# Inside an attention chunk: residue outermost, key block innermost

## The chip, the cores and the metric

The kernel runs on one core of a Trainium2 chip. The metric is device time of one launch in microseconds; 3923.4 us is the median of three runs of the kernel before (3923.32 to 3928.79).

The engines named here are PE (matrix products), DVE (vector), ACT (activations), POOL (GpSimd) and SP, which here only issues transfers. SBUF is the working memory, PSUM the memory that PE writes its sums to.

## The reference

The program is a chain of four layers on an input of 4 x 1024 tokens of 128 features, each an attention-like part and a feed-forward part with a residual and a layer norm. The change lies in the attention of layer 1, which attends not over tokens but over the 64 channels within each head of each token:

```python
H, C = (16, 64)
Q = (x @ Wq + bq).reshape(b, s, H, C) * inv_sqrt_c
K = (x @ Wk + bk).reshape(b, s, H, C)
V = (x @ Wv + bv).reshape(b, s, H, C)
scores = jnp.einsum('bshq,bshk->bshqk', Q, K)
mask = jnp.triu(jnp.ones((C, C), dtype=bool), 1)
scores = jnp.where(mask, -jnp.inf, scores)
w = jax.nn.softmax(scores, axis=-1)
attn = jnp.einsum('bshqk,bshk->bshq', w, V)
return attn.reshape(b, s, HID) @ Wo + bo
```

Each score is the product of two numbers, q of channel `q` and k of channel `k`, for `k <= q`. For 4096 tokens, 16 heads and 64 x 65 / 2 pairs there is one product, one subtraction of a row maximum, one exponential, one product with v, and two sums over k: the denominators and the numerators. No matrix product makes the scores; they are elementwise work.

## The kernel before, in words

**Tiling of the attention.** There are 32 tiles of 128 tokens, each cut into two units of 64 tokens, 64 units in all. A unit puts 32 tokens times 4 residues on the 128 partitions, and two such sets (`S = 2`) beside each other. A key channel is written `k = 4 n + r`: `n` is the key block (0 to 15), `r` the residue (0 to 3, `R = 4`). The partition group `i` of 32 holds the keys of residue `i`. So an operation over 128 partitions treats four keys of one block at once, one in each partition group.

**Tiles.** `qr` holds the queries of a unit, copied to all four partition groups, as (s, head, 64 channels) on the free axis; `mr` holds the row maxima in the same way. `kvr` is a PSUM bank with keys and values of eight key blocks (`half` 0 or 1), innermost axis the block. `ringe` is one long SBUF tile used as a ring: each chunk of scores takes a piece and gives it back when its numerator sum is done. `den` and `num` are PSUM banks with the sums, as 8 heads x 64 channels; two head halves and two sets fill four groups of 32 partitions.

**Chunks.** The generator `feed` (line 894) goes through 17 chunks a unit, in the order of line 898. An "n" chunk takes key block n against all later queries `q >= 4 (n + 1)`, where no mask is needed. A "d" chunk (two a unit, `i` = 0 and 1) takes, for eight key blocks at once, the queries that lie in the same block as the keys: 32 (s, head) rows x 8 blocks x 4 query residues = 1024 elements a partition. In a d chunk the mask matters: a key of residue `i` counts only for query residues `r >= i`. It is applied as a bias column of the exponential, `beyond[:, r]`, which holds a large negative number in the partition groups that must not count; so a d chunk needs four exponentials of 256 elements, one for each `r`.

**What happens to a chunk.** `feed` issues the first product, `ringe = qr * k`, on DVE (line 935; two of the n chunks of a unit on POOL, line 933). The generator `rest` (line 949) then issues: the subtraction `ringe - mr` on POOL (line 963); the exponential in place on ACT (line 973 for d chunks, line 975 for the others); the den sum on PE (line 981), by `add_up`, which multiplies with a 0/1 matrix that adds the four partition groups, in four calls, into `den[.., q0 : q0 + nq]`; the second product `ringe * v` in place on DVE (line 986); and the num sum on PE (line 998) by the same `add_up`. Sums of chunks keep their order through counters.

Before the change a d chunk lies in the ring as (row, block n, residue r), with r innermost, the order in which `qr`, `mr`, `den` and `num` hold their channels. The exponential of one `r` then takes every fourth element.

**Other places named.** `maxima` (line 808) writes `lo` (lines 814 to 817), a PSUM bank, through an output pattern in which neighbouring elements of the matmul land four floats apart; `queries` (line 799) writes a bank of the same size in contiguous order.

**What sets the order.** Every engine call goes through a recording wrapper (line 60), which is why the profile gives all of them the line L60; groups are told apart by tiles. The generators of all layers are merged by a planner (`Order`, line 138): it keeps a modelled clock for each engine, a modelled duration for each call (`length`, line 90), and issues next whatever can start first. The other layers run as three chains beside the attention. In `length`, an ACT call with an SBUF operand whose innermost step is more than one element is charged 1.05 ns more an element (lines 114 and 115); DVE's terms (103 to 108) and POOL's (121 to 124) do not ask for the step, only for a step of zero on POOL. The engines execute their queues in the order thus written out.

Of the kernel before, what the change touches and what calls it, by code (L numbers as in the profile page):

```python
# [14 lines left out]
AF = mybir.ActivationFunctionType  # L15
# [5 lines left out]
P = 128  # L21
# [8 lines left out]
H, C, R, S, NK = 16, 64, 4, 2, 16  # L30
SH = S * H
# [106 lines left out]
class Order:  # L138
# [28 lines left out]
    def part(self, ap):  # L167
        n = self.owner(ap)
        cols, piece = self.halved.get(n, (0, 0))
        return f"{n} part {ap.offset % cols // piece}" if cols else n  # L170
# [149 lines left out]
class Model:  # L320
# [573 lines left out]
    def feed(self):  # L894

        order = [("d", 1), *(("n", n) for n in range(8, NK - 1)), ("d", 0), *(("n", n) for n in range(8))]
        f = lambda tt: tt.rearrange("p s h c -> p (s h) c")
        count = 0  # L900
        for unit in self.units:
            seen = set()
            for kind, i in order:
                half = i if kind == "d" else i // 8
                if half not in seen:
                    seen.add(half)
                    yield "DVE", self.when(
                        lambda: unit.get("ready") and unit["half"][half],
                        lambda: max(self.order.until(unit["kvr"][half]), self.order.until(unit["qr"])),
                    )  # L910
                kk, vv = (unit["kvr"][half][:, x].rearrange("p s h n -> p (s h) n") for x in (0, 1))
                if kind == "d":
                    sh = [P, SH, 8, R]
                    part = lambda tt: f(tt)[:, :, 32 * i : 32 * i + 32].rearrange("p a (n r) -> p a n r", r=R)
                    kk, vv = (z[:, :, :, None].to_broadcast(sh) for z in (kk, vv))
                    q0, nq = 32 * i, 32
                    shape = lambda tt: tt.rearrange("p (a n r) -> p a n r", n=8, r=R)
                else:
                    q0 = R * (i + 1)
                    nq = C - q0  # L920
                    sh = [P, SH, nq]
                    part = lambda tt: f(tt)[:, :, q0:]
                    kk, vv = (z[:, :, i % 8, None].to_broadcast(sh) for z in (kk, vv))
                    shape = lambda tt, nq=nq: tt.rearrange("p (a q) -> p a q", q=nq)
                shared = (kind, i) in SHARED
                yield "POOL" if shared else "DVE", self.when(
                    lambda: self.ering.can(SH * nq), lambda: self.ering.back(SH * nq)
                ), True
                et = self.ering.take(SH * nq)
                e = shape(et)  # L930
                qk = part(unit["qr"]), kk
                if shared:
                    self.g.tensor_tensor(e, qk[0], unit["ks"][i][:, :, None].to_broadcast(sh), ALU.mult)
                else:
                    self.v.tensor_tensor(e, *qk, ALU.mult)
                self.asked(unit)
                what = dict(first=(kind, i) == order[0], last=(kind, i) == order[-1], q0=q0, nq=nq, half=half)
                rest = self.rest(unit, count, kind, et, shape, part(unit["mr"]), vv, **what)
                self.order.spawn(rest, "rest", self.order.latest)
                count += 1  # L940

# [7 lines left out]
    def rest(self, unit, count, kind, et, shape, m, vv, first, last, q0, nq, half):  # L949
        e = shape(et)  # L950
        rows = et.rearrange("p (s h q) -> p s h q", s=S, q=nq)

        def add_up(name):
            for hb in range(2):
                for s in range(S):
                    at = 32 * (S * hb + s)
                    self.pe.matmul(
                        unit[name][at : at + 32, :, q0 : q0 + nq], lhsT=self.k["rep"][:, 0:32],
                        rhs=rows[:, s, 8 * hb : 8 * hb + 8, :], start=first, stop=last,
                    )  # L960

        yield "POOL"
        self.g.tensor_tensor(e, e, m, ALU.subtract)
        unit["subs"] -= 1
        if unit["subs"] == 0:
            self.drop(unit["mr"])
            if unit is self.units[-1]:
                self.retire("mr", "hc", "big")
        yield "ACT"
        if kind == "d":  # L970

            for r in range(R):
                self.s.activation(e[:, :, :, r], e[:, :, :, r], AF.Exp, bias=self.k["beyond"][:, r : r + 1])
        else:
            self.s.activation(et, et, AF.Exp)

        turn = lambda: self.summed == count
        yield "PE", self.free("den", also=turn) if first else self.when(turn)
        if first:
            unit["den"] = self.new("den", 8, C)  # L980
        add_up("den")
        self.summed += 1
        if last:
            self.order.spawn(self.invert(unit), "close", self.order.latest)
        yield "DVE", self.when(lambda: self.valued == count)
        self.v.tensor_tensor(e, e, vv, ALU.mult)
        self.valued += 1
        unit["uses"][half] -= 1
        if unit["uses"][half] == 0:
            self.drop(unit["kvr"][half])  # L990
            if unit is self.units[-1] and len(self.slots["kvr"]) == 2:
                self.retire("kvr", "bg")
                self.most = 3
        turn = lambda: self.done == count
        yield "PE", self.free("num", also=turn) if first else self.when(turn)
        if first:
            unit["num"] = self.new("num", 8, C)
        add_up("num")
        self.done += 1
        self.ering.give(self.order.latest)  # L1000
        self.order.place = self.done / (17.0 * 2 * TPG)
        if self.order.place == NG:
            self.divide(self.ering.ap, "b", "b", "c")
        if last:
            self.order.spawn(self.close(unit), "close", self.order.latest)
# [1080 lines left out]
```

## Time and profile before

| what | value |
|---|---|
| median of three runs | 3923.4 us |
| the profiled execution | 3929.3 us, its span 3927.5 us |
| mean granted TensorE clock | 0.912 |
| DVE busy over the span | 3167.7 us (81%) |
| PE busy | 3096.5 us (79%) |
| POOL busy | 2922.0 us (74%) |
| ACT busy | 2628.2 us (67%) |
| DMA, mean rate | 85 GB/s |

The span is the time from the first to the last instruction of one profiled execution; the median comes from runs of their own. A group row of the profile names line, engine, operation, the tile written, the tiles read and the shape, then busy time and the mean duration of one, then how long the engine was idle just before and what ended that idle time. A row of a tile's own view gives shortest, median and longest duration in ns. A row of waits gives who waited for whom, total us, how often, and the longest.

A d chunk in the trace, from 2013.98 us: DVE's product of 1024 elements, from 2015.28 POOL's subtraction, from 2017.70 ACT's four exponentials in 2.83 us, from 2019.05 eight matmul records of the den sum in 0.64 us, from 2019.83 DVE's second product in 1.22 us, and from 2021.97 the num sum in 0.62 us.

### The profile page before, as it was taken

The page shows a single profiled execution, that of the slowest core. Times are in us where ns is not written, and L with a number is a line of the kernel's source. Part 1 is how long each engine was busy: PE and PEld are TensorE (multiplying, and loading weights), DVE is VectorE, ACT ScalarE, POOL GpSimd, SP SyncE. Part 2 cuts the span into 40 slices and gives each one's busy share as a digit, 9 for nine tenths or more (in the row PEclk, how much of TensorE's full clock was granted, in tenths as well). Part 3 has the DMA queues.
Part 4 walks back from the last instruction along what each step waited for, and adds up shares of the span by engine and source line. Part 5 has one row for each costly group of instructions (what it writes and reads, how often), then busy time and mean ns, then how long its engine had stood idle before and what let it go on. Part 6 is the DMA issues. An engine that isn't in the chain of part 4 may idle for free.

```text
span 3927.5 us, 130511 instructions
## 1 busy us (share of the span) xinstructions
PE 3096.5 (79%) x56496; PEld 1636.6 (42%) x56496; DVE 3167.7 (81%) x3988; ACT 2628.2 (67%) x5206; POOL 2922.0 (74%) x1320
## 2 busy tenths in 40 slices
PE   5577676777788887978888987978878888879872
PEld 2233232433344553544444553544444444436552
DVE  2888898899898889899888889889998988983321
ACT  4567565667667875777667875677766786666531
POOL 0779996999788887799788987788978987870000
PEclk8789788988899998999999999999999999989986
DMA  2322122212213333243423334243433334523564
GB/s 68 80 72 50 44 57 61 63 44 52 50 50 100 84 95 82 75 119 80 103 70 94 97 87 99 61 109 87 108 88 75 94 94 102 140 74 81 162 151 99
DMA packets 374136, 334.05 MB, mean 85 GB/s; under 512 B 196332, under 2 KB 304172, under 8 KB 373560
## 3 DMA queue, kind: packets, MB, share of 16 engines
q1 hardware_dynamic: 364216, 292.15, 30.0%
q0 software_dynamic: 9344, 33.56, 2.9%
q8 instruction: 442, 7.24, 0.8%
q14 instruction: 134, 1.10, 0.1%
HBM read 149.16 MB, written 42.21 MB: 49 GB/s over the span
## 4 chain that ended last, share of the span: by engine, by line
PE 27%; DVE 25%; ACT 17%; POOL 16%; issue 10%; DMA 4%; SPq 1%; DVEq 0%; POOLq 0%; ACTq 0%
DVE ringe L60 17%; POOL ringe L60 15%; PE bg L60 14%; ACT ringe L60 8%; PE den L60 6%; PE num L60 5%; DVE bg L60 4%; PE kvr L60 2%; ACT ha L60 2%; ACT b L60 1%; ACT x L60 1%; DVE a L60 1%; SPq L60 1%; ACT L60 1%; DVE b L60 1%
## 5 line engine op out<-in xcount | busy, mean ns | idle before, releaser
L60 POOL TENSOR_TENSOR ringe<-ringe,mr 128x1024 f32<-128x1024 f32 (+14 forms) x1088 | 2558.0, 2389 | 466.1 <-DVE ringe L60 346.4
L60 DVE TENSOR_TENSOR ringe<-ringe,kvr 128x1024 f32<-128x1024 f32 (+14 forms) x1102 | 1291.3, 1202 | 201.6 <-PE den L60 183.4
L60 ACT ACTIVATE ringe<-ringe 128x768 f32<-128x768 f32 (+14 forms) x964 | 1001.2, 1056 | 593.7 <-POOL ringe L60 590.6
L60 DVE TENSOR_TENSOR ringe<-qr,kvr 128x1024 f32<-128x1024 f32 (+12 forms) x960 | 1102.3, 1184 | 60.1 <-PE num L60 31.2
L60 PE MATMUL den<-ringe,cst 128*32 128x256 f32 (+7 forms) x8744 | 700.8, 419 | 263.6 <-ACT ringe L60 215.5
L60 PE MATMUL num<-ringe,cst 128*32 128x256 f32 (+7 forms) x8728 | 702.7, 411 | 213.8 <-DVE ringe L60 204.2
L60 PEld LDWEIGHTS den<-ringe,cst 128*32 128x32 f32 x8744 | 238.8, 115 | 573.0 <-ACT ringe L60 353.5
L60 PEld LDWEIGHTS num<-ringe,cst 128*32 128x32 f32 x8728 | 233.6, 114 | 539.3 <-DVE ringe L60 399.7
L60 ACT ACTIVATE ringe<-ringe,cst 128x256 f32<-128x256 f32 x512 | 357.2, 782 | 64.2 <-POOL ringe L60 63.9
L60 POOL TENSOR_TENSOR ringe<-qr,ks 128x896 f32<-128x896 f32 (+1 forms) x128 | 288.3, 2252 | 48.0 <-DMA mr<-t 23.4
L60 PE MATMUL bg<-xT,a 128*32 128x512 f32 (+1 forms) x1952 | 253.3, 616 | 31.3 <-DMA a<-w 9.2
L60 DVE TENSOR_TENSOR_SCAN bg<-ends,bg 128x512 f32<-128x512 bf16 x128 | 154.9, 1217 | 44.9 <-PE bg L60 43.4
L60 PE MATMUL kvr<-wkv,xT 128*32 128x256 f32 x2048 | 149.6, 413 | 31.9 <-DVE ringe L60 30.6
L60 PE MATMUL bg<-a,ha 128*32 128x128 f32 x4736 | 160.2, 276 | 14.6 <-ACT ha L60 14.4
L60 PEld LDWEIGHTS bg<-a,ha 128*32 128x32 f32 x4736 | 127.8, 111 | 35.8 <-ACT ha L60 18.1
L60 ACT COPY b<-bg 128x512 f32<-128x512 f32 (+2 forms) x217 | 96.6, 452 | 57.3 <-PE bg L60 53.1
L60 PE MATMUL bg<-xT,b 128*32 128x128 f32 (+1 forms) x3536 | 128.4, 285 | 8.2 <-ACT aT L60 4.8
L60 ACT ACTIVATE ha<-bg,cst 128x512 f32<-128x512 f32 (+1 forms) x151 | 97.6, 678 | 52.8 <-PE bg L60 52.6
L60 ACT ACTIVATE b<-cst,little 128x128 f32<-128x128 f32 x384 | 122.2, 397 | 0.0
L60 PEld LDWEIGHTS bg<-xT,b 128*32 128x32 f32 x3536 | 102.3, 114 | 35.3 <-issue 14.8
L60 PEld LDWEIGHTS bg<-xT,a 128*32 128x32 f32 x1952 | 61.5, 116 | 131.1 <-issue 61.2
L60 PE MATMUL bg<-b,cst 128*32 128x512 f32 (+1 forms) x800 | 107.4, 608 | 1.6 <-ACT b L60 0.9
(660 smaller groups left out, 4450.5 us busy)
## 6 DMA issues: line engine op xcount, KB each, us to landing
qr<-q SPq DMA_DIRECT2D x512, 128.0 KB
mr<-t SPq DMA_DIRECT2D x512, 128.0 KB
c<-in_f_Wdn SPq DMA_DIRECT2D x53, 256.0 KB
tu<-gt SPq DMA_DIRECT2D x25, 512.0 KB
c<-tu SPq DMA_DIRECT2D x200, 64.0 KB
td<-gt SPq DMA_DIRECT2D x24, 512.0 KB
c<-td SPq DMA_DIRECT2D x96, 128.0 KB
a<-in_f_W SPq DMA_DIRECT2D x37, 256.0 KB
```

Of the source, the lines that this page charges most:

```text
L60: return f(*args, **kw)
```

## The change

In a d chunk the element order in the ring becomes (row, residue r, block n), with n innermost. The exponential of one `r` then takes runs of eight neighbouring elements. `qr`, `mr`, `den` and `num` keep their order; so the d chunk's product reads `qr`, and its subtraction reads `mr`, with a step of four floats (16 bytes) between neighbours, and the two sums write `den` and `num` with that step. `kvr` is read with the block innermost and a repeat over r, where before the repeat was innermost. The n chunks are as they were. The planner's `length` is untouched.

```diff
                 if kind == "d":
-                    sh = [P, SH, 8, R]
-                    part = lambda tt: f(tt)[:, :, 32 * i : 32 * i + 32].rearrange("p a (n r) -> p a n r", r=R)
-                    kk, vv = (z[:, :, :, None].to_broadcast(sh) for z in (kk, vv))
+                    sh = [P, SH, R, 8]
+                    part = lambda tt: f(tt)[:, :, 32 * i : 32 * i + 32].rearrange("p a (n r) -> p a r n", r=R)
+                    kk, vv = (z[:, :, None, :].to_broadcast(sh) for z in (kk, vv))
                     q0, nq = 32 * i, 32
-                    shape = lambda tt: tt.rearrange("p (a n r) -> p a n r", n=8, r=R)
+                    shape = lambda tt: tt.rearrange("p (a r n) -> p a r n", n=8, r=R)
...
         rows = et.rearrange("p (s h q) -> p s h q", s=S, q=nq)
+        turned = (lambda t: t.rearrange("p h (n r) -> p h r n", r=R)) if kind == "d" else (lambda t: t)
...
                     self.pe.matmul(
-                        unit[name][at : at + 32, :, q0 : q0 + nq], lhsT=self.k["rep"][:, 0:32],
+                        turned(unit[name][at : at + 32, :, q0 : q0 + nq]), lhsT=self.k["rep"][:, 0:32],
                         rhs=rows[:, s, 8 * hb : 8 * hb + 8, :], start=first, stop=last,
                     )
...
             for r in range(R):
-                self.s.activation(e[:, :, :, r], e[:, :, :, r], AF.Exp, bias=self.k["beyond"][:, r : r + 1])
+                self.s.activation(e[:, :, r], e[:, :, r], AF.Exp, bias=self.k["beyond"][:, r : r + 1])
```

## The prediction

> **What bounds the kernel now.** I began with busy time by engine over the stretch in which the attention runs (its ring tile is written from 102 to about 3520 us), because the last 400 us hold other layers and would blur the shares.
>
> ```profile
> core 0: us, PE busy (x) PEld busy (x) DVE busy (x) ACT busy (x) POOL busy (x), PEclk, DMA share, GB/s
> 100.00:3520.00 3420.00, 2746.08 (x48483) 1397.75 (x48479) 3031.38 (x3587) 2400.09 (x4524) 2891.68 (x1279) 0.92 0.32 81
> ```
>
> In these 3420 us DVE is busy 88.6%, POOL 84.6%, PE 80.3%, ACT 70.2%. DVE is nearest to being the bound, POOL close behind, ACT has the most room. Next the waits and the last chain:
>
> ```profile
> ACT ringe L60 <- POOL ringe L60: 654.5, 446, 16.8
> POOL ringe L60 <- DVE ringe L60: 346.4, 94, 34.9
> DVE ringe L60 <- PE den L60: 195.1, 144, 5.4
> ```
> ```profile
> PE 27%; DVE 25%; ACT 17%; POOL 16%; issue 10%; DMA 4%; SPq 1%; DVEq 0%; POOLq 0%; ACTq 0%
> ```
>
> ACT waits for POOL, POOL waits for DVE, and DVE waits little, mostly for the den sum that must have read a chunk before DVE overwrites it. So DVE sets the pace, and a microsecond added to it counts nearly in full, while one saved on ACT counts only where DVE stands behind it. The chain passes through all engines, so no edit counts exactly at its own size.
>
> **The change, part by part.** There are 64 units with two d chunks each: 128 d chunks of 128x1024. No instruction is added or removed in kind: per chunk still one product on DVE, one subtraction on POOL, four exps on ACT, a den sum on PE, the second product on DVE, a num sum on PE. What changes is the step in bytes of their operands. Before, only the exps have a step of 16 bytes (every fourth float, read and written). After, the exps read and write runs of 8 floats; the first product reads qr every 16 bytes, the subtraction reads mr every 16 bytes, and the sums write den and num every 16 bytes. The rows:
>
> ```profile
> L60 ACT ACTIVATE ringe<-ringe,cst 128x256 f32<-128x256 f32 x512 | 357.2, 782 | 64.2 <-POOL ringe L60 63.9
> L60 ACT ACTIVATE ringe<-ringe 128x256 f32<-128x256 f32 x68 | 28.4, 418 | 10.4 <-POOL ringe L60 9.3
> L60 ACT ACTIVATE ha<-bg,cst 128x512 f32<-128x512 f32 x144 | 94.3, 688 | 52.3 <-PE bg L60 52.2
> L60 ACT ACTIVATE b<-bg 128x512 f32<-128x512 f32 x98 | 57.8, 592 | 27.3 <-PE bg L60 24.7 <-issue 1.8 <-ACT xp L60 0.7
> L60 DVE TENSOR_TENSOR ringe<-qr,kvr 128x1024 f32<-128x1024 f32 x192 | 231.1, 1211 | 37.8 <-ACT ks L60 28.5 <-PE num L60 9.1
> L60 DVE TENSOR_TENSOR ringe<-ringe,kvr 128x1024 f32<-128x1024 f32 x192 | 232.2, 1212 | 30.6 <-PE den L60 26.9 <-ACT ha L60 2.6 <-ACT last L60 0.2
> L60 POOL TENSOR_TENSOR ringe<-ringe,mr 128x1024 f32<-128x1024 f32 x192 | 456.4, 2391 | 73.1 <-DVE ringe L60 40.9 <-PE bg L60 13.0 <-PE num L60 10.9
> L60 POOL TENSOR_TENSOR ringe<-ringe,mr 128x1536 f32<-128x1536 f32 x64 | 222.8, 3482 | 2.7
> L60 POOL TENSOR_TENSOR ringe<-qr,ks 128x1536 f32<-128x1536 f32 x64 | 177.8, 2778 | 22.7 <-PE num L60 21.6 <-ACT x L60 1.0
> ```
>
> *ACT.* The strided exp takes 782 ns for 256 elements; a contiguous ringe activation of that size 418 ns without a bias column. A bias column costs 688 - 592 = 96 ns (the two PSUM rows). A contiguous exp with bias is then 514 ns, so the stride costs 268 ns, 1.05 ns for an element. 512 x 0.268 = 137 us leave ACT. Bounds: 0, if runs of 8 do no better, to 512 x (782 - 418) = 186 us. I take 137: nearly all of it is cover that ACT had. Its worth is bounded by the wait before the second product, 26.9 us behind den in the row above (64 other chunks share it).
>
> *DVE, first product.* No row of before has a DVE operand in SBUF with such a step. From below: 0, if DVE at 1211 / 1024 = 1.18 ns an element hides the fetch. From above: the only strided row there is, ACT's 1.05 ns an element, makes 1024 x 1.05 = 1.07 us a chunk and 128 x 1.07 = 137 us. ACT's excess may come from its strided write rather than its read, which the row cannot separate; but DVE's pace is as near to one element a step as ACT's (1811 ns for 1920 elements), so I see nothing that would hide a slower fetch, and take 137 us. The other operand in PSUM costs nothing either way: the broadcast moves from the innermost place to the one before it, and a DVE product that reads PSUM element by element (rd<-num,rd, 685 ns for 512) is as fast as one with an innermost broadcast (ringe<-ringe,kvr, 677 for 512). The second product is contiguous in ringe before and after: 0.
>
> *POOL, subtraction.* Again no row. Bounds 0 to ACT's 1.05 ns an element, 137 us. That POOL pays for operands one by one is seen in its rows: with one operand broadcast, 1536 elements take 2778 ns instead of 3482, 0.46 ns an element less. A slower fetch then shows, and I take 137 us. POOL goes to (2892 + 137) = 3029 us of busy time.
>
> [...]
>
> *PE.* The strided output has a row. The maxima's matmul writes its bank with the same 16-byte step (line 815), the queries' matmul writes 512 contiguous:
>
> ```profile
> L60 PE MATMUL bg<-wkv,xT x512: 591/592/1062, 87.5 to 3348.4; 128*32 128x512 f32 x171
> L60 PE MATMUL bg<-wq,xT x512: 591/592/1061, 78.7 to 3322.6; 128*32 128x512 f32 x171
> ```
>
> Shortest and median are equal: 0 on PE. It is cheap only while that holds; the rival below has the price.
>
> [...]
>
> *Order.* The planner drops its stride term (line 115) for the exps, 0.27 us each, and has no such term for DVE or POOL (lines 103 to 108, 121 to 124). So all five queues are reordered, SP's transfers among them, on durations that are about 1 us too short twice per d chunk; what stands behind a late product in DVE's queue (other chunks' products, scans, residual sums) is late with it, and POOL waits for it. I charge nothing for that and leave it in the width.
>
> **Sum.** DVE +137, less up to 27 that ACT's shorter exps take from its wait: +110. POOL's 137 goes beside it, since at 3029 of some 3530 us it stays at 86%, under DVE's 3168 (90%). On the profiled span: 3927.5 + 110 = 4037.5. That execution took 3929.3 and the median of three is 3923.4, so on the median 4033 us. From half the DVE price to the full one with 57 us of mistimed order behind it: 3975 to 4090 for this case alone.
>
> **Rivals.**
> - *Neither DVE nor POOL pays* (the end on the other side). ACT's excess is then its strided write, and after the change every write to SBUF is in runs. For it: DVE's writes are contiguous as before. Against it: ACT's row has both, and POOL pays visibly for operands. ACT loses 137 of 2628 us; of its 17% of the chain (668 us) that share is 35 us, and the wait behind den gives 27. I take -20: 3903, and 3888 at most. It decides as soon as a strided 128x1024 product stays under about 1.3 us.
> - *POOL alone pays.* POOL reaches 3029, DVE's present 3031, so both stand at 88.6%. POOL's wait for DVE (346 us) takes up about half: +69, less the 20 from ACT: about 3972.
> - *The sums on PE pay too*: the change does move a stride where accumulating cost may differ from the maxima's single write. One sum of a d chunk takes 0.62 us in the timeline; twice that on 256 sums is +159 us on PE, 2905 of busy time. Half of it on the path on top of the forecast: about 4113. Against it are the two equal rows.
>
> **How the numbers follow.** The forecast (DVE pays, POOL with it or not) 0.64; POOL alone 0.13; PE too 0.05; neither 0.18. A measurement of this kernel tells about 0.2% (7.8 us) from no change. Of the neither case 0.13 is faster by more, 0.04 within, 0.01 slower because of the new order; all else is slower: 0.83. The range is 3910 to 4090: below lie most of the neither case (0.11), above the PE case and the forecast's upper tail (0.09).
>
> **What would show it.** Exp on ringe<-ringe,cst near 514 ns; of the qr,kvr 128x1024 group a third (its 192 mix 128 d and 64 n chunks) still at 1.21 us and the rest near 2.28, mean near 1.9; the ringe,mr 128x1024 group's mean near 3.1; den and num 128x256 unchanged near 0.41; DVE's share of the attention's stretch near 90% and that stretch near 3530 us. The forecast is wrong if the DVE product stays at 1.21, or if DVE's added time appears and the stretch does not grow.

## The result and the profile after

The changed kernel takes 3934.61 us (median of 10 runs, 3931.51 to 3938.57) against 3927.84 us for the kernel before (10 runs): ratio 1.0021, 95% interval [1.0011, 1.003]. It is slower by 6.8 us, where 110 were forecast. The profiled execution took 3933.5 us with a span of 3931.8.

First the groups whose operands changed their step, in the view of groups by shape of the changed kernel:

```profile
L60 ACT ACTIVATE ringe<-ringe,cst 128x256 f32<-128x256 f32 x512 | 218.0, 499 | 109.4 <-POOL ringe L60 109.2
L60 DVE TENSOR_TENSOR ringe<-qr,kvr 128x1024 f32<-128x1024 f32 x192 | 338.6, 1767 | 31.7 <-ACT ks L60 17.5 <-PE num L60 11.9 <-DMA mr<-t 2.2
L60 DVE TENSOR_TENSOR ringe<-ringe,kvr 128x1024 f32<-128x1024 f32 x192 | 233.1, 1216 | 17.9 <-PE den L60 14.2 <-ACT ringe L60 2.1 <-ACT bg L60 0.8
L60 POOL TENSOR_TENSOR ringe<-ringe,mr 128x1024 f32<-128x1024 f32 x192 | 526.9, 2755 | 124.4 <-DVE ringe L60 110.9 <-PE den L60 4.4 <-DMA qr<-q 3.1
L60 PE MATMUL den<-ringe,cst 128*32 128x256 f32 x1536 | 131.5, 416 | 76.5 <-ACT ringe L60 53.0 <-ACT rd L60 5.8 <-POOL ringe L60 4.9
```

An exponential fell from 782 to 499 ns: 512 x 0.283 = 145 us less on ACT. The qr,kvr group mixes 128 d chunks with 64 n chunks; with the n chunks at their old 1211 ns, a d product takes (192 x 1767 - 64 x 1211) / 128 = 2045 ns, 0.83 us more, 107 us on DVE. A subtraction takes (192 x 2755 - 64 x 2391) / 128 = 2937 ns, 0.55 us more, 70 us on POOL. The second product reads its `kvr` operand with the repeat moved in the same way, and it kept its duration (1216 ns, before 1212); so the 0.83 us belong to the step in `qr`. The sums kept theirs within 5 ns. So every part moved in the direction forecast, yet the total hardly did. Busy time in the same 3420 us of the attention, by engine as in the prediction's first table:

```profile
core 0: us, PE busy (x) PEld busy (x) DVE busy (x) ACT busy (x) POOL busy (x), PEclk, DMA share, GB/s
100.00:3520.00 3420.00, 2734.38 (x48365) 1389.94 (x48357) 3116.36 (x3561) 2266.02 (x4502) 2949.66 (x1275) 0.92 0.32 81
```

DVE is busy 3116 us there (91.1%, before 88.6%), POOL 2950, ACT 2266. In the same stretch DVE is busy 85 us longer, in time in which it was idle before. How far the attention itself grew is seen from when the last first product of a unit starts, in the tile's own view of before and then of the changed kernel:

```profile
L60 DVE TENSOR_TENSOR ringe<-qr,kvr x960: 269/1210/2153, 102.0 to 3513.7; 128x1024 f32<-128x1024 f32 x64, 128x256 f32<-128x256 f32 x64, 128x1664 f32<-128x1664 f32 x64
L60 DVE TENSOR_TENSOR ringe<-qr,kvr x960: 261/1347/2203, 102.3 to 3532.1; 128x1024 f32<-128x1024 f32 x64, 128x256 f32<-128x256 f32 x64, 128x1664 f32<-128x1664 f32 x64
```

It starts 18 us later, where some 110 were forecast, and the rest of the program behind it takes 400 us against 414. The waits say where some of DVE's time went:

```profile
ACT ringe L60 <- POOL ringe L60: 746.9, 520, 9.3
POOL ringe L60 <- DVE ringe L60: 307.9, 94, 12.4
DVE ringe L60 <- PE den L60: 141.4, 134, 4.0
```

DVE waits 141 us for den sums, before 195; POOL waits 308 us for DVE, before 346; ACT waits 747 us for POOL, before 655. The chain of the changed kernel is traced over only 56% of its span, so its shares can't be set beside those of before:

```profile
PE 19%; DVE 13%; ACT 8%; POOL 7%; issue 5%; DMA 3%; SPq 1%; DVEq 0%; POOLq 0%; ACTq 0%
```

### The profile page after: what moved, and what is told of

Its sections match the earlier page's. It is cut to its first block, busy times and chain, and to the rows that moved or that the text cites. A ratio compares the mean times of both kernels' runs of the same rounds, so it can differ in the third digit from the quotient of the medians.

```text
span 3931.8 us, 130457 instructions
## 1 busy us (share of the span) xinstructions
PE 3087.4 (79%) x56496; PEld 1630.5 (41%) x56496; DVE 3269.1 (83%) x3988; ACT 2502.5 (64%) x5206; POOL 2991.7 (76%) x1320
## 4 chain that ended last, share of the span: by engine, by line
PE 19%; DVE 13%; ACT 8%; POOL 7%; issue 5%; DMA 3%; SPq 1%; DVEq 0%; POOLq 0%; ACTq 0%
PE bg L60 11%; DVE ringe L60 9%; POOL ringe L60 7%; PE den L60 4%; PE num L60 3%; ACT ringe L60 3%; DVE bg L60 2%; PE kvr L60 2%; ACT b L60 1%; SPq L60 1%; ACT ha L60 1%; ACT L60 1%; ACT x L60 0%; DMA mr<-td 0%; DVE b L60 0%
## 5 line engine op out<-in xcount | busy, mean ns | idle before, releaser
L60 POOL TENSOR_TENSOR ringe<-ringe,mr 128x1024 f32<-128x1024 f32 (+14 forms) x1088 | 2627.2, 2451 | 399.6 <-DVE ringe L60 307.9
L60 DVE TENSOR_TENSOR ringe<-qr,kvr 128x1024 f32<-128x1024 f32 (+12 forms) x960 | 1211.7, 1298 | 58.7 <-PE num L60 38.9
L60 PEld LDWEIGHTS num<-ringe,cst 128*32 128x32 f32 x8728 | 225.6, 113 | 570.5 <-DVE ringe L60 450.3
L60 ACT ACTIVATE ringe<-ringe,cst 128x256 f32<-128x256 f32 x512 | 218.0, 499 | 109.4 <-POOL ringe L60 109.2
L60 PE MATMUL bg<-b,cst 128*32 128x512 f32 x832 | 110.6, 604 | 5.0 <-ACT b L60 4.9
```

The lines of the kernel that those rows point to most:

```text
L60: return f(*args, **kw)
```

## The experiments

The change does two things at once: it moves the step between engines, and it lets the planner write a new order. All experiments rest on keeping these apart. A flag around the four exponentials tells the planner what to charge for them, whatever their real step is; nothing else in it looks at what the change touches. With 1 it charges the old term and gives every queue the old order, instruction by instruction; with 2 it charges none and gives the order of the changed kernel. The traces bear this out: in every run said to be in one of the two orders the queues of DVE, ACT, POOL and SP hold the same instructions in the same order, and PE's agree in over 99.5% of their places. The runs with one part alone mix up elements and are no usable kernels; they serve to price the part.

```diff
-        if any(not in_psum(a) and a.free_size() > 64 and a.ap[-1][0] > 1 for a in aps[:2]):
+        if BEYOND[0] == 1 or BEYOND[0] == 0 and any(not in_psum(a) and a.free_size() > 64 and a.ap[-1][0] > 1 for a in aps[:2]):
             long += 1.05e-3 * n
...
+            BEYOND[0] = 1
             for r in range(R):
...
+            BEYOND[0] = 0
```

Before was run again beside each group of runs: 3928.7 us for the first four, 3925.5 for the next, 3927.9, 3924.8 and 3924.5 for the others. Ratios are against it.

### Layout and order apart

> The changed layout with every queue in the order of the kernel before (the planner still charges the four exponentials of a d chunk with their old stride term). Theory 'order': the new layout alone costs what the prediction said and the new order gave it back: +60 to +110 us over before. Theory 'trade': the layout's loss on DVE and POOL is paid back by ACT's gain whatever the order: within 15 us of before. Theory 'slack': DVE's added time fits into its own idle time: also within 15 us, told apart from 'trade' by the two runs with one part alone.

3969.2 us, ratio 1.0102 [1.0088, 1.0117]: +40 us. The last first product starts at 3557.5 us, 44 later than before. The layout alone costs far more than the change did, less than theory "order" said and more than "trade" and "slack" allowed.

> The layout of before with every queue in the order of the changed kernel (the planner no longer charges the stride term for the four exponentials, which still pay it on the chip). Theory 'order': the new order is the better one, so 50 to 100 us below before. Theories 'trade' and 'slack': the order is worth little, within 15 us of before (a few us slower, since ACT's time is now underrated by 1.1 us a chunk).

3923.4 us, ratio 0.9991 [0.9981, 1.0001]: with the old layout the new order can't be told from the old one. With the new layout it is worth 3969.2 - 3934.6 = 35 us.

### One part at a time, in the old order

ACT alone:

```diff
-                self.s.activation(e[:, :, :, r], e[:, :, :, r], AF.Exp, bias=self.k["beyond"][:, r : r + 1])
+                run = et.rearrange("p (a r n) -> p a r n", n=8, r=R)[:, :, r]
+                self.s.activation(run, run, AF.Exp, bias=self.k["beyond"][:, r : r + 1])
```

> In the order of before, only the four exponentials take runs of eight; products, subtractions and sums stay as before, so biases meet elements of other residues and the output is not the reference's. ACT should lose 0.28 us x 512 = 145 us of busy time, DVE and POOL nothing. Theory 'trade': 30 to 70 us faster than before. Theory 'slack': ACT's time was cover, 0 to 10 us faster.

3896.7 us, ratio 0.9918 [0.9905, 0.9931]: 32 us faster. ACT's time was not only cover. But the wait from which the prediction took its worth, the second product's behind den, fell only from 26.9 to 22.3 us:

```profile
L60 DVE TENSOR_TENSOR ringe<-ringe,kvr 128x1024 f32<-128x1024 f32 x192 | 233.5, 1218 | 28.5 <-PE den L60 22.3 <-ACT ringe L60 3.0 <-ACT ha L60 2.1
```

POOL's wait for DVE fell more, from 346 to 318 us.

DVE alone, on the first product of d chunks (written in more lines here than in the kernel):

```diff
+                if kind == "d":
+                    q, k = unit["qr"].rearrange("p s h c -> p (s h) c")[:, :, q0 : q0 + 32], unit["kvr"][half][:, 0].rearrange("p s h n -> p (s h) n")
+                    qk = q.rearrange("p a (n r) -> p a r n", r=R), k[:, :, None, :].to_broadcast([P, SH, R, 8])
+                    e = et.rearrange("p (a r n) -> p a r n", n=8, r=R)
```

> In the order of before, only the first product of a d chunk reads qr with the 16-byte step (and kvr with the repeat outside); subtraction, exponentials and sums take the elements as before, so they are mixed up and the output is not the reference's. DVE should gain 0.83 us x 128 = 107 us of busy time. Theory 'trade': 40 to 107 us slower than before. Theory 'slack': DVE hides it, 0 to 15 us slower.

3964.6 us, ratio 1.0092 [1.0079, 1.0105]: +36 us. The group of this run shows the full price on the engine:

```profile
L60 DVE TENSOR_TENSOR ringe<-qr,kvr 128x1024 f32<-128x1024 f32 x192 | 338.4, 1770 | 35.9 <-ACT ks L60 26.4 <-PE num L60 9.4
```

107 us more on the engine that is busiest, and 36 us more in the end. Both theories had this outside or at the edge of what they said: the part is neither hidden nor counted in full.

POOL alone, on the subtraction:

```diff
-        self.g.tensor_tensor(e, e, m, ALU.subtract)
+        if kind == "d":
+            m = m.rearrange("p a n r -> p a r n")
+            ee = et.rearrange("p (a r n) -> p a r n", n=8, r=R)
+            self.g.tensor_tensor(ee, ee, m, ALU.subtract)
+        else:
+            self.g.tensor_tensor(e, e, m, ALU.subtract)
```

> In the order of before, only the subtraction of a d chunk reads mr with the 16-byte step; the other steps take the elements as before, so they are mixed up and the output is not the reference's. POOL should gain 0.55 us x 128 = 70 us of busy time. If the parts add up to the new layout in the old order (+40 of which DVE +36 and ACT -32), POOL alone is 25 to 45 us slower than before. If POOL hides behind DVE, as the prediction had it, 0 to 10 us slower and the parts don't add up.

3958.7 us, ratio 1.0088 [1.0071, 1.0105]: +33 us for 70 us of busy time.

```profile
L60 POOL TENSOR_TENSOR ringe<-ringe,mr 128x1024 f32<-128x1024 f32 x192 | 526.8, 2757 | 75.9 <-DVE ringe L60 50.2 <-PE bg L60 11.4 <-ACT a1nm L60 11.2
```

POOL does not hide behind DVE.

PE alone, den and num of d chunks through `turned`:

> In the order of before, only the den and num sums of the d chunks are written with the 16-byte step in PSUM (the sums go to channels of other residues, so the output is not the reference's). Theory 'free', by the equal rows of the maxima's and queries' matmuls: den and num 128x256 unchanged near 0.41 us, time within 5 us of before. [...]

3930.0 us, ratio 1.0009 [0.9999, 1.0019]: +4 us, and by the interval between 0 and 7. The groups of the d and n chunks together:

```profile
L60 PE MATMUL den<-ringe,cst 128*32 128x256 f32 x1536 | 132.6, 416 | 72.1 <-ACT ringe L60 34.8 <-ACT last L60 13.1 <-ACT ks L60 11.7
L60 PE MATMUL num<-ringe,cst 128*32 128x256 f32 x1536 | 127.6, 404 | 36.7 <-DVE ringe L60 31.4 <-DVE rd L60 4.4
```

Before they were 411 and 402 ns. But in the run with DVE alone, whose sums are written without a step, they were 416 and 406:

```profile
L60 PE MATMUL den<-ringe,cst 128*32 128x256 f32 x1536 | 132.1, 416 | 64.0 <-ACT ringe L60 33.9 <-ACT last L60 14.4 <-ACT ks L60 6.1
L60 PE MATMUL num<-ringe,cst 128*32 128x256 f32 x1536 | 128.2, 406 | 45.3 <-DVE ringe L60 40.4 <-DVE rd L60 4.3
```

So the step in PSUM costs nothing that can be seen here.

The four parts add up: 36 + 33 - 32 + 4 = 41 us, and the layout as a whole cost 40. So they do in the attention: its last first product moves by 40, 32, -32 and 5 us, 45 in all, against 44.

### Where on DVE the step is paid

The changed kernel, with this in place of the first product's operands (again in more lines than in the kernel):

```diff
+                if kind == "d":
+                    q, k = unit["qr"].rearrange("p s h c -> p (s h) c")[:, :, q0 : q0 + 32], unit["kvr"][half][:, 0].rearrange("p s h n -> p (s h) n")
+                    qk = q.rearrange("p a (n r) -> p a n r", r=R), k[:, :, :, None].to_broadcast([P, SH, 8, R])
+                    e = et.rearrange("p (a r n) -> p a n r", n=8, r=R)
```

> The changed kernel in its own order, but the first product of a d chunk goes through its elements as before: it reads qr contiguously with the repeat of kvr innermost, and writes ringe with a step of 8 floats (32 bytes). Nothing is left out. Theory 'read pays': the product is back at 1.21 us and the kernel 25 to 45 us below the changed kernel, at 3890 to 3910. Theory 'write pays too': the product stays near 2.0 us or above and the time within 10 us of the changed kernel's 3935.

3931.1 us, ratio 1.0016 [1.0005, 1.0026]: no gain over the changed kernel that can be told.

```profile
L60 DVE TENSOR_TENSOR ringe<-qr,kvr 128x1024 f32<-128x1024 f32 x192 | 333.7, 1742 | 28.2 <-ACT ks L60 17.6 <-PE num L60 7.6 <-DMA qr<-q 2.7
```

A d product takes (192 x 1742 - 64 x 1211) / 128 = 2008 ns. A write with a step of 32 bytes costs DVE 0.80 us, as much as a read with 16 (0.83).

### What an order is worth

The planner told of DVE's and POOL's real price:

```diff
-        return long, 0.14
+        return long + (0.81e-3 * n if any(not in_psum(a) and a.free_size() > 64 and a.ap[-1][0] > 1 for a in aps) else 0.0), 0.14
...
-        return 0.145 + 2.13e-3 * n, 0.08
+        return 0.145 + 2.13e-3 * n + (0.53e-3 * n if any(a.free_size() > 64 and a.ap[-1][0] > 1 for a in aps) else 0.0), 0.08
```

> The changed layout with a planner that also charges the 16-byte step to DVE (0.81 ns an element) and POOL (0.53 ns), so every queue gets an order made for the real durations. If part of the loss is stalls from durations rated too short: 10 to 30 us below the changed kernel (3905 to 3925). If an order is worth only a few us by chance: within 10 us of 3935.

3942.9 us, ratio 1.0048 [1.0031, 1.0066], 8 us above the changed kernel: a model with these two prices made no better order.

> As the run with ACT alone, but in the order of the changed kernel (the same elements are mixed up, the output is not the reference's). Base: the old layout in the new order, 3923. Theory 'fit' (the new order is made for short exponentials): ACT's 145 us are worth clearly more than the 32 us they were worth in the old order, 50 to 65, so 3858 to 3875. Theory 'room' (the new order gives DVE and POOL more slack): worth about 32 again, 3885 to 3897.

3859.3 us, ratio 0.9827 [0.9814, 0.9841]. Against the old layout in that order (3923.4) ACT's part is worth 64 us, twice as much as in the old order.

> As the run with DVE alone, in the order of the changed kernel (elements mixed up in the same way). Theory 'fit': DVE's 107 us cost about 36 again, 3955 to 3965. Theory 'room': they cost 10 to 22 us here, 3933 to 3945.

3958.7 us, ratio 1.008 [1.0065, 1.0094]: +35 us.

> As the run with POOL alone, in the order of the changed kernel (elements mixed up in the same way). Theory 'fit': POOL's 70 us cost about 33 again, 3950 to 3960. Theory 'room': they cost 8 to 20 us here, 3931 to 3943.

3950.8 us, ratio 1.0054 [1.0039, 1.007]: +27 us. DVE and POOL cost nearly the same in both orders; only ACT's saving is worth more in the order planned for short exponentials, as "fit" said. In this order 64 us come back where 62 go out, which is how the change ends near zero (11 us above the old layout in that order, where the parts with PE's 4 add up to about 2). In the attention alone the parts add up here too: against the old layout in this order the last first product moves by -65 (ACT), 43 (DVE) and 30 us (POOL), with PE's 5 by 13 in all, and by 14 with the changed layout.

The same with half of the old term charged, a further order, with three layouts:

> The changed layout in a fourth order: the planner charges the four exponentials half of the old stride term. Theory 'fit': between the new order's 3935 and the old order's 3969, near 3950. Theory 'scatter' (orders differ by chance): anywhere from 3915 to 3975, and outside 3935 to 3969 it speaks against 'fit'.

3919.4 us, ratio 0.9982 [0.9973, 0.9991]: outside what "fit" allows, and even a little faster than before.

> The old layout in the order of the half term, as a base for the next run. Theory 'scatter' (an order is worth up to 20 us by chance, with the old layout as with the new): 3885 to 3915, since this order is 16 us better than the new one with the new layout. Theory 'fit' alone: 3922 to 3930, as the two orders so far.

3888.4 us, ratio 0.9912 [0.9896, 0.9929]: the layout of before, not one instruction changed, 36 us faster by its order alone.

> Only the exponentials in runs of eight, in the order of the half term (elements mixed up as in the other runs of ACT alone, the output is not the reference's). ACT's 145 us were worth 32 us in the order planned for strided exponentials and 64 in the one planned for short ones. Theory 'fit': between them, 40 to 56 below the run before this one. Theory 'scatter': anything, also outside 32 to 64.

3841.1 us, ratio 0.9795 [0.9778, 0.9811]: ACT's part is worth 47 us here, between 32 and 64. Fit and scatter are both there: between its best and its worst of three orders each layout differs by 40 to 56 us, and beside that ACT's saving is worth the more, the shorter the planner took the exponentials to be. Three orders are few for the second part of this. In the table, by how much each differs from the old layout in the same order:

| order, by the term charged for the exponentials | old layout | changed layout | ACT alone |
|---|---|---|---|
| full (order of before) | 3928.7 | 3969.2 (+40) | 3896.7 (-32) |
| half | 3888.4 | 3919.4 (+31) | 3841.1 (-47) |
| none (order of the change) | 3923.4 | 3934.6 (+11) | 3859.3 (-64) |

One rival runs beside all this: the granted clock is not the same in these kernels. Its mean over a kernel's runs is 0.908 to 0.910 for before, 0.906 for the changed layout in the old order, 0.911 for the changed kernel and 0.919 for ACT alone in the new order. Among runs of the same kernel, 0.001 more clock goes with 1.1 us less (a slope pooled over 196 runs, each against the mean of its own group; correlation -0.55). By that, as an estimate, the clock goes with 5 of the 35 us between the two orders of the changed layout, and with 2, 4 and 10 us of ACT's 32, 47 and 64. So it does not carry these differences, but it narrows the last comparison to about 30, 43 and 54. Whether the clock makes a run shorter or follows from how the work lies is not shown.

### A step of 8 bytes

```diff
+                    part = lambda tt: [f(tt)[:, :, 32 * i : 32 * i + 32].rearrange("p a (n b c) -> p b a n c", b=2, c=2)[:, b] for b in range(2)]
...
+                    shape = lambda tt: tt.rearrange("p (b x c) -> p b x c", b=2, c=2)
...
+                    for b in range(2):
+                        self.v.tensor_tensor(et.rearrange("p (b a n c) -> p b a n c", b=2, n=8, c=2)[:, b], qk[0][b], kk, ALU.mult)
...
+                self.s.activation(e[:, r // 2, :, r % 2], e[:, r // 2, :, r % 2], AF.Exp, bias=self.k["beyond"][:, r : r + 1])
```

The subtraction and the sums are split in the same two halves, and nothing is left out. The planner charges no stride term for the exponentials in this run.

> A complete version with no 16-byte step: the ring holds a d chunk as (residue pair, row, block, residue within the pair), so exponentials step by 8 bytes and qr and mr are read in runs of two floats. The first product, the subtraction and each sum are issued twice with half the elements (DVE +0.14 us, POOL +0.20 us a chunk, PE +0.18 us a sum, from the rows of 512 elements and 128 columns). If a step of 8 bytes costs nothing: exponentials near 0.50 us, products 0.68, subtractions 1.29 us, and the kernel 15 to 50 us below before, 3880 to 3915. If 8 bytes pay like 16: products near 1.09 us, no gain, 3930 to 3970.

3873.0 us, ratio 0.9869 [0.9848, 0.9889]: 52 us faster than before. Its groups, and behind them two of before with contiguous operands:

```profile
L60 ACT ACTIVATE ringe<-ringe,cst 128x256 f32<-128x256 f32 x512 | 237.9, 539 | 28.1 <-POOL ringe L60 27.5
L60 DVE TENSOR_TENSOR ringe<-qr,kvr 128x512 f32<-128x512 f32 x320 | 208.0, 683 | 37.4 <-ACT ks L60 31.8 <-PE num L60 5.5
L60 POOL TENSOR_TENSOR ringe<-ringe,mr 128x512 f32<-128x512 f32 x320 | 411.9, 1308 | 58.4 <-DVE ringe L60 54.7 <-DMA qr<-q 2.7 <-PE den L60 0.8
L60 DVE TENSOR_TENSOR ringe<-qr,kvr 128x512 f32<-128x512 f32 x64 | 43.3, 677 | 0.0
L60 POOL TENSOR_TENSOR ringe<-ringe,mr 128x512 f32<-128x512 f32 x64 | 82.8, 1294 | 0.9 <-DVE ringe L60 0.8
```

The products read two floats, skip two, and take 683 ns for 512 elements, where contiguous ones take 677; the subtractions 1308 against 1294; the exponentials with a step of 8 bytes 539, against 499 in runs of eight and 782 with a step of 16. So runs of two floats cost DVE and POOL about 1%, and ACT pays 40 ns of its 283 at a step of 8 bytes. Two halves are cheaper than the step that they avoid: 1366 ns against 2045 on DVE, 2616 against 2937 on POOL; on PE they are dearer, two den sums of 288 ns for one of 411.

> The complete version with steps of 8 bytes, in the order that comes out when the planner charges its exponentials the full old stride term (the instructions differ from before, so this is near the old order but not it). If the gain of 52 us is the layout's: 3860 to 3900 again. If it was the luck of one order: 3905 to 3935.

3835.8 us, ratio 0.9777 [0.9761, 0.9792]: 89 us below before.

> The same with half of the stride term charged. If the gain is the layout's: 3840 to 3900. If it was the luck of one order: 3905 to 3935.

3908.2 us, ratio 0.9964 [0.9951, 0.9977]. All three orders are below before, by 16 to 89 us, and their mean (3872) is below that of the old layout in its three orders (3914). But against the old layout planned with the same term they are 93 us faster (full), 50 faster (none) and 20 slower (half), and 72 us lie between three orders of the same instructions. So a gain of the layout itself is likely but not shown by three orders; that the instructions with a step are dearer than their halves is shown by the rows.

## Why the prediction was wrong

**ACT's saving, 137 us of busy time:** right, 145 measured. Its worth was given as up to 27 us, from the wait before the second product, the rest as cover. Measured: 32 in the old order, 64 in the new. The bound from one wait was too low, and its path was wrong in the old order: the kernel gained 32 us while that wait fell by 5 (in the new order it fell by 24, from 44.3 to 20.1, of the 64). ACT also works for the other layers' chains, which may have gained too; which waits carry the rest stays open.

**DVE +137 and POOL +137 us:** both pay, as forecast, but less: 107 and 70. ACT's 1.05 ns an element was too high a price for them; DVE pays 0.81 (0.83 us / 1024), POOL 0.53. On a subtraction with one such operand of two that is 0.55 us on 2.39, 23%.

**The step that failed: "DVE sets the pace, and a microsecond added to it counts nearly in full".** 107 us added to DVE alone cost 36 in the old order and 35 in the new, a third (in the attention alone 40 and 43). The profile showed DVE at 88.6% of the stretch, which left 389 us idle, and a chain that gives DVE only 25% of the time; the prediction read the first and set the second aside. No single engine sets the pace here: time added to DVE, to POOL or taken from ACT each showed, and none in full. In the old order the runs gave 36 / 107 = 34% for DVE, 33 / 70 = 47% for POOL and 32 / 145 = 22% for ACT; the chain's shares (25, 16 and 17%) were too low for all three, but far nearer for DVE than the 100% that was used.

**"POOL's 137 goes beside it":** wrong for the same reason. Alone it cost 33 and 27 us.

**PE 0:** right for the rows, and +4 us (0 to 7) for the time. The rival at 4113 us took a strided sum at twice its length; no run shows that, den and num took 416 and 404 ns against 411 and 402 before.

**The order, "I charge nothing for that":** the other failing term. With the changed layout the new order took 35 us less than the old one, so of the 40 us that the layout costs, 7 were left. Its width was put at 57 us of loss and nothing of gain. Why this order suits the changed layout is shown in part only: ACT's saving is worth 32 us more in it, DVE's and POOL's parts cost nearly the same.

**The range and the sign.** The time lies inside the range of 3910 to 4090, but below the 3975 to 4090 of the forecast's own case; what was left of the range was there for the rivals. (3975 is about what half of the 110 gives; half of DVE's price less the 27 would give 3965.) "Slower" came true by the luck of the order: planned with half of the term, the same layout takes 3919.4 us, 8 less than before. The sign that the prediction named, DVE's added time there and the stretch not growing, came in part: the added time is there, and the stretch grew by 18 us of some 110.

**The rivals.** "Neither pays" had 3903, and the rows refute it: both engines pay. "POOL alone pays" at 3972 is refuted by the same rows. None of the cases had all parts paying and giving back about the same sum.

## What to carry to other kernels

Don't price an edit at its full size because it falls on the busiest engine, when others are nearly as busy: here, with DVE at 88.6% and POOL at 84.6%, a third of DVE's added time counted, about 40 to 50% of POOL's, a fifth to under a half of what ACT lost, each above the engine's share of the last chain. Where a planner writes the order, run a change in the old order as well as in the new one, and take several orders before a difference of 1% is put down to the change. Of a step of 16 bytes that must be somewhere, ask first whether runs of two floats will do: here the two halves in such runs took 1366 ns on DVE where one product with the step took 2045, and 2616 against 2937 on POOL.

## What the runs showed of the hardware

A step in SBUF cost DVE 0.8 ns an fp32 element, read at 16 bytes (2045 against 1211 ns on 1024) or written at 32 (2008), while the other operand came from PSUM; POOL 0.53 ns for one operand read at 16 bytes (2937 against 2391 ns); ACT 1.1 ns (782 - 499 ns on 256) for read and write together at 16 bytes. Runs of two floats cost DVE and POOL 1%, and a step of 8 bytes cost ACT 0.16 ns (539 - 499 on 256).
